# Rulers made ahead of the gathers, borders of edges in eight pieces, and another order of the last steps

## The chip, the core and the metric

The kernel runs on one core of a Trainium2 chip. The metric is the device time of one execution in microseconds (us). The engines of the core are PE (TensorE, matrix products; PEld is its weight load), DVE (VectorE), ACT (ScalarE), POOL (GpSimd) and SP (SyncE); each has a queue of its own and works through it in order. Transfers (DMAs) are issued by SP, ACT and POOL.

## The reference

A layer of a graph network over N = 12500 nodes of F = 128 features, with E = 212500 edges sorted by their target `dst`, and 8 heads of 16:

```python
h = maximum(layernorm(x), 0)
q = h @ Wq.T + bq;  k = edge_attr @ Wk.T + bk;  v = h @ Wv.T + bv
qs, qd = q[src], q[dst]
in_m, out_m, diag_m = sum(qs * k), sum(qd * k), sum(qs * qd)     # of each head
att = distance ** lam
score = (softmax over the edges of a node of in_m, out_m, diag_m, summed) * att
h = segment_sum(score[..., None] * v[dst], dst)
out = x + leaky_relu(h @ Wo.T + bo, 0.1)
```

So each edge needs the row of `q` of its source, which can be any of the 12500, and the row of `q` of its target, which lies near those of its neighbours in the list.

## The kernel before, in words

The edges lie in 416 blocks of 512. The list is cut into S = 5 stretches of G = 83 blocks (one block is left for the end); step g of the main loop does block t = g // 5 of stretch s = g % 5, so there are 415 steps (`end`). Three stages follow one another.

**First stage (lines 734 to 1014).** It makes `q` of all nodes, 98 tiles of 128 nodes in 25 groups of four. A loop over g from -2 to 34 does, for each group: `rectify` (ACT, line 921, four operations), `turn_h` (PE transposes, ACT copy, line 931), `nodes_q` (PE products, DVE sum, line 940, and SP's store of the group to `q_table`, line 942), then `ready` (mean and deviation to scale and shift) and `count_upto` (DVE statistics, line 886, eight groups ahead). Groups 25 to 34 are ten blocks of edges whose rows of `x` were gathered before `q` existed (`RAW`; 40 gathers on POOL, each behind a DVE instruction of its group). `side[g]` and the conditions on `r = g - GN` hang other work on the loop: the turning of sources and weights of edges, `edges_3` (the distance of each edge's target from the first of its block, line 832, and where each block begins), `edges_4` (borders between targets, lines 841 to 846), and `terms_of` (each `q` as a sum of three bfloat16 terms, nine units, lines 953 to 958; `put_terms` stores them, line 662). `show` makes rulers (constant patterns) from two POOL `iota`s (lines 752 and 755) and two DVE operations (757, 758). At g = 24 the gathers from `q_table` begin.

**Main loop (lines 1493 to 1552).** POOL gathers four times 128 rows of `q` for each step (`gather`, line 691), 20 steps ahead (`LOOK`) and behind the products of an earlier step. PE turns and projects the block's features (1154, 1163), spreads the targets' `q` from a window of 38 nodes (`win`, 645, and a one-hot matrix, 1171); DVE multiplies (1184, 1185) and adds up the heads (1190). One and two blocks later the softmax follows: `scan_on` (1244), `scan_back` (1262), `turn_max` (1332), `powers` (1340, 1341), `weigh_powers` (1352), `show_ends` (1366 to 1370), `to_rows` (PE, 1380) and `put_rows` (1396), which writes a stretch's 38 rows of sums to DRAM. Where the rows go is read into SP's registers by `fetch` (626). Pairs of finished nodes are completed on the way (`Nodes`).

**Last steps (lines 1555 to 1609).** Blocks 81, 82 and the odd one, 83, go through the softmax one after the other; then the sums of the last nine units (`rest`, five pairs; `load_sums`, lines 1061 and 1063) are read back, turned into scores together (`scores_of`, 1030 to 1036), and each pair is weighted with its `v` (`weigh`, 1096), turned (1080, 1083), multiplied with `Wo` (1088, 1107), added to `x` (1112, 1113) and stored (1119). `hold` computes `v` of a pair into a bank of PSUM. `last_pair` is a pair of nodes that is finished between.

The order of each engine is written out by hand: `pin` chains an instruction behind the one pinned before on the same engine:

```python
if engine in pinned:
    tc.add_manual_dep(inst.ins, pinned[engine], ... reason="in order")
pinned[engine] = inst.ins.name
```

What isn't pinned (the rulers of `show`, the register loads of `fetch`) is placed by the framework.

Of the kernel before, what the change touches and what calls it, by code (L numbers as in the profile page):

```python
# [21 lines left out]
FAR = 1e30  # L22
# [450 lines left out]
def ordered_path(ctx: ExitStack, tc: tile.TileContext, flag, x, src, dst, edge_attr, edge_weight,  # L473
# [144 lines left out]
    def fetch(t):  # L618

        if t >= T:  # L620
# [5 lines left out]
        _, base_v[t] = nc.values_load_multi_w_load_instructions(  # L626
            bases[0:1, t:t + (S - 1) * G + 1:G], engines=[mybir.EngineType.SP], min_val=0, max_val=N - 1,
            skip_runtime_bounds_check_because="the indices of nodes are below N")
        st[t] = dict(far=far)
# [104 lines left out]
    with tc.tile_pool(name="prep", bufs=1) as prep, \  # L734
# [14 lines left out]

        def show():  # L750
            of = prep.tile([K4, JN, S, W], F32, name="of_f", tag="of", bufs=2)
            nc.gpsimd.iota(of, pattern=[[1, JN], [JN, S], [0, W]], base=1, channel_multiplier=-1,
                           allow_small_or_imprecise_dtypes=True)
            row = prep.tile([1, JN, S, W], F32, name="of_row", tag="of", bufs=2)
            nc.gpsimd.iota(row, pattern=[[0, JN], [0, S], [1, W]], base=1, channel_multiplier=0,
                           allow_small_or_imprecise_dtypes=True)
            nc.vector.tensor_scalar(shows, of, 0.0, -1.0, op0=ALU.is_equal, op1=ALU.mult)
            nc.vector.tensor_copy(shows[0:1], row)
# [63 lines left out]
        def edges_2():  # L822
            turn_edges(weight, att_t)

        def edges_3():
            for i, lo in enumerate((1, BE, HEAD, 0)):
                pin(nc.vector.tensor_copy(marks[:, i], dst_r[:, lo:lo + (RB - 1) * BE + 1:BE]))
            pin(nc.sync.dma_start(base_d.rearrange("(r a) -> r a", a=RB),
                                  dst_r[:, 1:RC + 1:BE]))
            rel_b = of_tile().rearrange("r (a e) -> r a e", a=RB)  # L830
            for a in range(RB):
                pin(nc.vector.tensor_scalar(
                    rel_b[:, a].rearrange("r (j p) -> r p j", j=JN),
                    dst_r[:, 1 + a * BE:1 + (a + 1) * BE].rearrange("r (p j) -> r p j", j=JN),
                    marks[:, 0, a:a + 1], 1.0, op0=ALU.subtract, op1=ALU.add))
# [144 lines left out]
        for g in range(-2, GN + max(RAW, len(new) + 1)):  # L980
# [12 lines left out]
            if g in side:  # L993
                side[g]()
# [13 lines left out]
            if r == 3:  # L1008
                fetch_places(0)
# [645 lines left out]
```

## Time and profile before

| | |
|---|---|
| three runs | 2204.27, 2207.11, 2220.55 us; median 2207.11 |
| profiled execution | 2203.87 us, of which the span is 2201.3 us |
| busy | PE 78%, DVE 89%, ACT 64%, POOL 72% |
| granted clock of TensorE | 0.796 of full speed |
| gathers from `q_table` on POOL | 1620, from 85.8 us to 2128.1 us |
| products with gathered rows on DVE | 415, from 120.9 us to 2132.2 us |

A row of the timeline reads: start in us, duration in us, engine, line, operation, output and inputs, shapes, count of merged instructions, and in brackets how long the engine sat idle before it and what ended that. A row of the groups reads: busy time, mean ns of one, idle time before. A row of the windows gives for each engine its busy time in that stretch.

### The profile page before, as it was taken

How to read it: one execution, taken by the hardware profiler on the slowest of the kernel's cores; microseconds unless marked ns; L12 is line 12 of the kernel's file. 1: busy time of each engine (PE TensorE's matmuls, PEld its weight loads, DVE VectorE, ACT ScalarE, POOL GpSimd, SP SyncE). 2: the span in 40 equal slices, each digit the busy share in tenths (PEclk: the TensorE clock that was granted, in tenths of full speed). 3: DMA queues.
4: the chain of work that ended last, by engine and by line, in shares of the span. 5: the costliest groups of instructions: out<-in, count | busy, mean ns of one | idle time of the engine just before them, and what ended most of it. 6: DMA issues, size and time to landing. Idle time of an engine off the chain costs nothing.

```text
span 2201.3 us, 34508 instructions
## 1 busy us (share of the span) xinstructions
PE 1708.5 (78%) x10337; PEld 1362.8 (62%) x10337; DVE 1958.7 (89%) x2140; ACT 1414.6 (64%) x2639; POOL 1595.4 (72%) x1676
## 2 busy tenths in 40 slices
PE   6767777777778786888788778877877888788875
PEld 4545656566566665666666666666665666666664
DVE  7858999999888999989999999999999998988893
ACT  6846666666666666666666766666666666666671
POOL 5677777777777777777777777777777777777750
PEclk9867888878877878777877887787788777877877
DMA  9585554555554555545555554555556545544531
GB/s 260 170 255 152 168 164 148 175 149 162 173 155 146 157 166 176 160 148 156 175 168 154 183 170 147 158 180 157 156 166 183 150 147 164 162 148 145 161 91 58
DMA packets 306062, 355.66 MB, mean 162 GB/s; under 512 B 118195, under 2 KB 225661, under 8 KB 305557
## 3 DMA queue, kind: packets, MB, share of 16 engines
q1 hardware_dynamic: 237258, 238.26, 35.1%
q0 software_dynamic: 53184, 108.92, 17.1%
q10 hardware_dynamic: 15424, 6.19, 1.1%
q8 instruction: 83, 1.36, 0.3%
q14 instruction: 113, 0.93, 0.1%
HBM read 321.34 MB, written 31.85 MB: 160 GB/s over the span
## 4 chain that ended last, share of the span: by engine, by line
PE 37%; DVE 31%; DMA 11%; issue 9%; ACT 4%; POOL 2%; SPq 1%; ACTq 0%; DVEq 0%; POOLq 0%
PE kq_ps L1163 13%; DMA qq<-q_table,src_i 10%; DVE lT L1190 10%; DVE prod L1185 10%; PE w_ps L1380 6%; DVE prod L1184 5%; PE eT_ps L1154 5%; PE kq_ps L1161 4%; DVE u L1244 3%; PE node_ps L1088 3%; PE kq_ps L1171 3%; POOL qq L691 2%; PE d_ps L1366 2%; PE l_ps L1211 1%; ACT relb L1148 1%
## 5 line engine op out<-in xcount | busy, mean ns | idle before, releaser
L691 POOL DMA_INDIRECT qq<-q_table,src_i x1620 | 1547.1, 955 | 494.1 <-issue 233.9
L1163 PEld LDWEIGHTS kq_ps<-wk,eT 128*128 128x128 f32 x3320 | 522.2, 240 | 377.1 <-issue 159.4
L1190 DVE TENSOR_REDUCE lT<-prod 128x192 f32<-128x3072 f32 (+1 forms) x249 | 702.1, 2819 | 8.6
L1163 PE MATMUL kq_ps<-wk,eT 128*128 128x128 f32 x3320 | 617.5, 343 | 7.5 <-ACT eT L1156 6.5
L1174 ACT COPY qd<-kq_ps 128x512 f32<-128x512 f32 x415 | 242.2, 584 | 417.0 <-PE kq_ps L1171 386.0
L1185 DVE TENSOR_TENSOR prod<-qq,kq_ps 128x1024 f32<-128x1024 f32 x415 | 503.2, 1213 | 5.9 <-issue 3.2
L1161 PE MATMUL kq_ps<-b,ones 3*128 3x512 bf16 x415 | 185.6, 447 | 223.0 <-DVE prod L1185 222.8
L1154 PE MATMUL eT_ps<-ident,ea 128*128 128x128 f32 x1660 | 323.5, 330 | 1.0 <-DVE qq L940 1.0
L1148 ACT ACTIVATE relb<-relb,before 114x512 bf16<-114x512 bf16 x415 | 302.6, 729 | 0.0
L1184 DVE TENSOR_TENSOR prod<-qd,kq_ps 128x512 f32<-128x512 f32 x415 | 279.5, 674 | 12.0 <-ACT qd L1174 6.8
L1149 ACT ACTIVATE oh<-relb 114x512 bf16<-114x512 bf16 x415 | 261.4, 630 | 13.6 <-ACT relb L1148 0.4
L1156 ACT COPY eT<-eT_ps 128x512 f32<-128x512 f32 x415 | 244.0, 588 | 37.7 <-PE eT_ps L1154 37.2
L1154 PEld LDWEIGHTS eT_ps<-ident,ea 128*128 128x128 f32 x1660 | 229.1, 175 | 1.1 <-DVE qq L940 1.1
L1380 PE MATMUL w_ps<-back,sel 128*114 128x144 f32 (+1 forms) x1344 | 213.7, 320 | 19.3 <-DVE back L1352 14.8
L1380 PEld LDWEIGHTS w_ps<-back,sel 128*114 128x114 f32 (+1 forms) x1344 | 205.6, 211 | 26.4 <-ACT h L1070 9.2
L1332 PE MATMUL m_ps<-ident,m 120*128 120x120 f32 x332 | 70.9, 347 | 170.3 <-DVE m L1262 167.8
L1171 PE MATMUL kq_ps<-win,oh 114*128 114x128 bf16 x1660 | 199.9, 255 | 2.6 <-DMA win<-q_table 2.6
L1341 ACT ACTIVATE back<-back 128x480 f32<-128x480 f32 x83 | 50.1, 604 | 201.9 <-DVE back L1340 201.9
L1244 DVE TENSOR_TENSOR_SCAN u<-far,u,l_ps 120x512 f32<-120x512 bf16 x82 | 104.7, 1276 | 78.2 <-PE l_ps L1211 77.0
L1171 PEld LDWEIGHTS <-oh 114*128 114x128 bf16 x1660 | 161.2, 118 | 15.5 <-issue 2.8
L1332 PEld LDWEIGHTS m_ps<-ident,m 120*128 120x128 f32 x332 | 50.7, 215 | 192.8 <-DVE m L1262 188.6
L1262 DVE TENSOR_TENSOR_SCAN m<-far_ps,head,u 120x512 f32<-120x512 f32 x81 | 103.1, 1273 | 0.0
(192 smaller groups left out, 1467.4 us busy)
## 6 DMA issues: line engine op xcount, KB each, us to landing
ea<-in_edge_attr_dram SPq DMA_DIRECT2D x83, 1280.0 KB
relb<-rel_d SPq DMA_DIRECT2D x83, 640.0 KB
qq<-q_table,src_i POOLq DMA_INDIRECT x1620
win<-q_table SPq DMA_DIRECT2D x415, 28.5 KB
far<-far_d SPq DMA_DIRECT2D x84, 120.2 KB
q_table<-more_q SPq DMA_DIRECT2D x40, 192.0 KB
sums<-rows SPq DMA_DIRECT2D x412, 7.1 KB
q_table<-xq SPq DMA_DIRECT2D x24, 256.0 KB
```

What stands on the lines that cost most here:

```text
L691: rows = pin(nc.gpsimd.indirect_dma_start(out=qq[:, j, :], out_offset=None, in_=x if g < RAW else q_table, in_offset=bass.IndirectOffsetOn ...
L1148: pin(nc.scalar.activation(d, d, AF.Abs, bias=before[:K3]))
L1149: pin(nc.scalar.activation(oh, d, AF.Relu, bias=1.0, scale=-1.0))
L1154: pin(nc.tensor.transpose(eT_ps[:, j, :], eas[g // S][:, g % S, j * F:(j + 1) * F], ident))
L1156: pin(nc.scalar.copy(eT, eT_ps))
L1161: pin(nc.tensor.matmul(k_ps, ones3, bk3, start=True, stop=False))
L1163: pin(nc.tensor.matmul(k_ps[:, j, :], eTs[g][:, j, :], wk, start=False, stop=(j == JN - 1)))
L1171: pin(nc.tensor.matmul(qd_ps[:, j, :], ohs[g][:, j * P:(j + 1) * P], d["win"][:, s, :], start=(j == 0), stop=(j == JN - 1)))
L1184: pin(nc.vector.tensor_mul(prod[:, :, 2, :], qds[g], kqs[g][:, 0]))
L1185: pin(nc.vector.tensor_mul(prod[:, :, 0:2, :], qqs[g][:, :, None, :].to_broadcast([P, JN, 2, F]), kqs[g].rearrange("p i j f -> p j i f")))
L1190: pin(nc.vector.tensor_reduce(lTs[t][:, :, lo:s + 1, :].rearrange("p j s c -> p j (s c)"), prods[0][:, :, :s + 1 - lo].rearrange("p j s i ...
L1380: pin(nc.tensor.matmul(w_ps[:, i].rearrange("p s c -> p (s c)"), d["sel"][:n, j, lo:lo + 3, :].rearrange("p s w -> p (s w)"), d["back"][:n ...
```

## The change

First stage: both `iota`s of the rulers are issued before the first gather, and the two DVE operations that use them are pinned. `edges_3` and `edges_4` are cut into four pieces each, one for each quarter of a row of blocks; one piece is issued at each g from 11 that has no other side work (11, 12, 14, 15, 18, 20, 21, 22). What ACT does for the borders (`edges_5`) comes at g = 24, the check of order (`edges_6`) at the end of the stage. The turning of weights (`edges_2`) is spread over four g. `fetch_places(0)` and `fetch(0)` come at r = 0. The tile `q3` gets five buffers for three, and its second cast moves from ACT to DVE.

Main loop: the window of the first block is fetched before the borders of the second. In the last five steps `select` and `show_ends` of the last three blocks are issued one a step; `v` of the first pair of `rest` and the turning of `last_pair` are issued in the last two steps. The register loads are pinned, and for the last three blocks ACT loads them too.

Last steps: `hold`, `powers`, `weigh_powers` and `to_rows` stand in another order; every second `put_rows` of the last three blocks is issued by ACT; `last_pair` gets its scores before the sums are loaded, and its end (`add_x`, with the sum on POOL) follows later; the scores of `rest` are made in two parts, of two pairs and of three.

```diff
@@ fetch
-        _, base_v[t] = nc.values_load_multi_w_load_instructions(
-            bases[0:1, t:t + (S - 1) * G + 1:G], engines=[mybir.EngineType.SP], ...
+        at = [mybir.EngineType.SP] + [mybir.EngineType.Activation] * (t >= G - 2)
+        loads, base_v[t] = nc.values_load_multi_w_load_instructions(
+            bases[0:1, t:t + (S - 1) * G + 1:G], engines=at, ...
+        for load_of in loads:
+            pin(load_of)
@@ first stage
+        of_f = prep.tile([K4, JN, S, W], F32, name="of_f", tag="of", bufs=2)
+        nc.gpsimd.iota(of_f, ...)
+        of_row = prep.tile([1, JN, S, W], F32, name="of_row", tag="of", bufs=2)
+        pin(nc.gpsimd.iota(of_row, ...))
+
         def show():
-            of = prep.tile([K4, JN, S, W], F32, name="of_f", tag="of", bufs=2)
-            nc.gpsimd.iota(of, ...)
-            row = prep.tile([1, JN, S, W], F32, name="of_row", tag="of", bufs=2)
-            nc.gpsimd.iota(row, ...)
-            nc.vector.tensor_scalar(shows, of, 0.0, -1.0, op0=ALU.is_equal, op1=ALU.mult)
-            nc.vector.tensor_copy(shows[0:1], row)
+            pin(nc.vector.tensor_scalar(shows, of_f, 0.0, -1.0, op0=ALU.is_equal, op1=ALU.mult))
+            pin(nc.vector.tensor_copy(shows[0:1], of_row))
...
-        def edges_2():
-            turn_edges(weight, att_t)
-        def edges_3():
...
-        def edges_4():
...
+        def edges_2(which):
+            turn_edges(weight, att_t, which)
+        def edges_3(a):
+            if a == 0:
+                for i, lo in enumerate((1, BE, HEAD, 0)):
+                    pin(nc.vector.tensor_copy(marks[:, i], dst_r[:, lo:lo + (RB - 1) * BE + 1:BE]))
+                pin(nc.sync.dma_start(base_d.rearrange("(r a) -> r a", a=RB),
+                                      dst_r[:, 1:RC + 1:BE]))
+                made["rel"] = of_tile().rearrange("r (a e) -> r a e", a=RB)
+            pin(nc.vector.tensor_scalar(made["rel"][:, a]..., dst_r[:, 1 + a * BE:1 + (a + 1) * BE]...,
+                marks[:, 0, a:a + 1], 1.0, op0=ALU.subtract, op1=ALU.add))
+            if a == RB - 1:
+                pin(nc.sync.dma_start(rel_d.rearrange("(r a) e -> r a e", a=RB), made["rel"]))
+                pin(nc.sync.dma_start(bases, base_d[None, :]))
+        def edges_4(a):
+            if a == 0:
+                made["cuts"] = of_tile()
+            part = slice(a * BE, (a + 1) * BE)
+            pin(nc.vector.tensor_tensor(made["cuts"][:, part], dst_r[:, 1:][:, part], dst_r[:, part],
+                                        op=ALU.is_gt))
+        def edges_5():
             far_b = of_tile()
-            pin(nc.scalar.mul(far_b, cuts, -FAR))
+            pin(nc.scalar.mul(far_b, made["cuts"], -FAR))
...
+        def edges_6():
+            pin(nc.vector.scalar_tensor_tensor(of_tile(), dst_r[:, 1:], 0.0, dst_r[:, :RC], op0=ALU.add,
                                                op1=ALU.is_lt, accum_out=worst))
...
-                q3 = q3s[u] = node.tile([P, 2, 3, F], BF, name="q3", bufs=3)
+                q3 = q3s[u] = node.tile([P, 2, 3, F], BF, name="q3", bufs=5)
...
-                pin(nc.scalar.copy(q3[:, :, 1, :], q))
+                pin(nc.vector.tensor_copy(q3[:, :, 1, :], q))
...
+        pieces = [(edges_3, a) for a in range(RB)] + [(edges_4, a) for a in range(RB)]
...
             if g in side:
                 side[g]()
+            elif g >= 11 and pieces:
+                f, a = pieces.pop(0)
+                f(a)
...
                 gather_few()
-                edges_3()
+                edges_5()
...
-            if r == 3:
+            if r == 0:
                 fetch_places(0)
-            if r == 4:
-                edges_4()
                 fetch(0)
-            if r == 6:
-                edges_2()
+            if 2 <= r < 2 + RB:
+                edges_2([r - 2])
+            if r == len(new):
+                edges_6()
@@ main loop
-            sel = st[t]["sel"] = work.tile([P, JN, S, W], F32, name="sel", bufs=3)
+            sel = st[t]["sel"] = work.tile([P, JN, S, W], F32, name="sel", bufs=4)
...
-                    pin(nc.sync.dma_start(
+                    pin((nc.scalar if t >= G - 2 and s % 2 else nc.sync).dma_start(
...
+        fetch_rows(0)
         fetch(1)
-        fetch_rows(0)
...
+            if t == G - 2 and 0 < s < 3:
+                select(G - 2 + s)
             if t == G - 1:
-                if 0 < s < 4:
-                    select(G - 3 + s)
-                elif s == 4:
-                    for i in (G - 2, G - 1, G):
-                        show_ends(i)
+                if s == 0:
+                    select(G - 2)
+                    show_ends(G - 1)
+                elif s == 1:
+                    show_ends(G)
+                elif s == 2:
+                    show_ends(G - 2)
...
+            if g == end - 2:
+                hold(rest[0], True)
+            if g == end - 1:
+                last_pair.turn(small([P, JN, P], "node_ps"))
+                more_banks()
@@ last steps
         turn_logits(G - 1)
-        last_pair.scores()
-        last_pair.turn(small([P, JN, P], "node_ps"))
+        last_pair.project_v(banks.pop(0))
         scan_on(G - 1)
-        hold(rest[0], True)
-        more_banks()
-        last_pair.project_v(banks.pop(0))
         scan_back(G - 2)
+        hold(rest[1])
         turn_max(G - 2)
         scan_on(G)
+        powers(G - 2)
         scan_back(G - 1)
         turn_max(G - 1)
+        weigh_powers(G - 2)
         scan_back(G)
         turn_max(G)
-        for t in (G - 2, G - 1, G):
-            powers(t)
-        for t in (G - 2, G - 1, G):
-            weigh_powers(t)
-        last_pair.weigh(last_pair.held)
-        for t in (G - 2, G - 1, G):
+        to_rows(G - 2)
+        powers(G - 1)
+        powers(G)
+        weigh_powers(G - 1)
+        weigh_powers(G)
+        put_rows(G - 2)
+        for t in (G - 1, G):
             to_rows(t)
             put_rows(t)
+        last_pair.scores()
+        last_pair.weigh(last_pair.held)
         for r, of in enumerate(rest):
             of.load_sums(ends_ab[:, r * JN:r * JN + of.n], of.more)
-        hold(rest[1])
...
-        last_pair.add_x(nc.vector)
-        last_pair.store()
...
+        end_scores(0, 2)
         for r in range(len(rest) + 2):
             if r < len(rest):
                 rest[r].weigh(rest[r].held)
+            if r == 1:
+                last_pair.add_x(nc.gpsimd)
+                last_pair.store()
+                end_scores(2, len(rest))
...
-                rest[r - 2].add_x(nc.vector)
+                rest[r - 2].add_x(nc.gpsimd if r == 2 else nc.vector)
```

`end_scores(lo, hi)` adds the second part of the sums of pairs lo to hi - 1 (DVE, the operation of line 1596) and calls `scores_of` for their tiles alone.

53 lines of the change are left out of this document (21 added, 32 removed).

## The prediction

> **What bounds the kernel now.** I read the page's totals first, then the tile view of `qq`, then what DVE waits for late in the main loop, then the timelines of the first 120 us and the last 75 us.
>
> ```profile
> PE 1708.5 (78%) x10337; PEld 1362.8 (62%) x10337; DVE 1958.7 (89%) x2140; ACT 1414.6 (64%) x2639; POOL 1595.4 (72%) x1676
> L691 POOL DMA_INDIRECT qq<-q_table,src_i x1620 | 1547.1, 955 | 494.1 <-issue 233.9
> ...
> L691 POOL DMA_INDIRECT qq<-q_table,src_i x1620: 940/947/2766, 85.8 to 2128.1; - x180
> L1185 DVE TENSOR_TENSOR prod<-qq,kq_ps x415: 1201/1212/1222, 120.9 to 2132.2; 128x1024 f32<-128x1024 f32 x139
> ...
> DVE prod L1185 <- DMA qq<-q_table,src_i: 2.5, 1, 2.5
> DVE prod L1185 <- issue: 1.5, 1, 1.5
> ```
>
> DVE looks like the bound at 89%, and POOL, at 72%, does not. But POOL's idle time is 494.1 / 1620 = 0.305 us ahead of each gather, so a gather costs 0.955 + 0.305 = 1.26 us, and 1620 of them take 2041 us: they run from 85.8 to 2128.1 us without a break. The last product starts 4.1 us behind the last gather, the first one 35 us behind the first. So DVE, a little quicker than four gathers a step (5.04 us), catches up during the loop and late in it waits for rows (the last two lines, from 1800 to 2100 us). It waits little, 4 us: there the two have the same pace, and an earlier stream is worth its full gain only if DVE starts earlier too. The loop's end is **the start of the gather stream plus 2041 us**. What the change does in the middle is hidden; two places count: what sets the start at 85.8 us, and the 73 us after 2128.1 us.
>
> ```profile
> 18.11 1.13 POOL L755 IOTA of_row<- 1x760 f32 x1
> 19.28 0.55 DVE L758 CAST shows<-of_row 1x760 bf16<-1x760 f32 x1 [6.66 <-POOL of_row L755]
> 19.75 2.20 DVE L886 BATCH_NORM_STATS2 stats<-xq 128x6 f32<-128x128 f32 x11
> ...
> 23.82 1.65 ACT L921 ACTIVATE xq<-xq,shift,inv 128x128 f32<-128x128 f32 x4 [0.82 <-DVE shift L909]
> ...
> 68.35 11.28 SPq L942 DMA_DIRECT2D q_table<-xq  x7
> ...
> 80.53 4.80 DVE L832 TENSOR_SCALAR of<-dst_r,marks 104x512 bf16<-104x512 int32 x4
> 80.76 4.69 POOL L691 DMA_INDIRECT qq<-in_x_dram,raw_i  x1 [0.30 <-issue]
> 85.76 0.95 POOL L691 DMA_INDIRECT qq<-q_table,src_i  x1 [0.31 <-DMA base_d<-dst_r]
> ...
> 96.57 2.28 DVE L841 TENSOR_TENSOR of<-dst_r 104x2048 bf16<-104x2048 int32 x1
> 97.78 1.89 POOL L691 DMA_INDIRECT qq<-q_table,src_i  x1 [0.30 <-issue]
> 100.88 2.29 DVE L846 SCALAR_TENSOR_TENSOR of<-dst_r 104x2048 bf16<-104x2048 int32 x1 [2.03 <-ACT of L843]
> 101.23 2.77 POOL L691 DMA_INDIRECT qq<-q_table,src_i  x1 [0.30 <-issue]
> ...
> 24.00:48.00 24.00, 22.20 (x133) 17.96 (x134) 19.75 (x85) 23.91 (x62) 11.24 (x12) 1.00 0.85 213
> 48.00:80.26 32.26, 28.50 (x185) 21.43 (x182) 27.98 (x120) 31.26 (x83) 15.02 (x17) 1.00 0.71 235
> 80.26:114.00 33.74, 22.89 (x123) 18.33 (x122) 25.99 (x64) 25.99 (x65) 27.34 (x22) 0.80 0.53 136
> ...
> GB/s 260 170 255 152 168 164 148 175 149 162 173 155 146 157 166 176 160 148 156 175 168 154 183 170 147 158 180 157 156 166 183 150 147 164 162 148 145 161 91 58
> ...
> xq<-in_x_dram SPq DMA_DIRECT2D x5, 896.0 KB
> L957 ACT CAST q<-xq 128x256 bf16<-128x256 f32 x9 | 3.7, 407 | 0.7 <-DVE xq L954 0.6
> ```
>
> Two things hold the start. DVE stands still for 6.66 us because the second ruler is queued on POOL behind eleven gathers; statistics, and ACT with them, wait. And the last gather from `x` takes 4.69 us for 0.95, and ends at 85.45 us just as DVE's four operations of line 832 do (80.53 + 4.80): while these run POOL does not get on. The gathers beside lines 841 and 846 are stretched in the same way.
>
> **The change part by part: the start.** *Rulers ahead.* POOL is free before its first gather, whose indices come from DVE, so the 1.13 us cost nothing there. The wait of 6.66 us goes. Line 757, until now done early, joins 758, so I take 5.9 us. Whether the features are there 6 us sooner the trace doesn't show; bounds 0 and 6.7. Ahead of the tiles that DVE takes next lie 1.8 MB of pieces of `x` (0.9 MB the last) and 0.6 MB of gathers, 9 us at the 260 GB/s of the page's first slice, so they should be. ACT is then the limit to 48 us (23.91 of 24), and keeps the 5.9 us.
>
> *Eight pieces.* They add to DVE, from g = 11 on (about 48 us now), 4.80 for line 832, 2.28 and four small overheads for 841 and 0.4 for the marks: 7.7 us. The window from 48 to 80.26 us has 32.26 - 27.98 = 4.3 us of idle DVE. So DVE becomes the limit of that stretch and ends it 3.4 us later; bounds 0 (other pauses are used) and 7.7 (none is). Net, `q` is complete 5.9 - 3.4 = 2.5 us sooner. The lock of 3.7 us falls among gathers from `x`, which are paced by DVE and have room (15.02 of 32.26 us). The last of the seven stores to `q_table` is issued near 79.3 us now (they end at 68.35 + 11.28) and would be at 77; the stream starts about 80.5 instead of 85.76: **5 us sooner** (3 to 9).
>
> *Within the stream.* Line 841's stretch (1.89 - 0.95) goes, line 846 stays (at the end of the stage) with its 1.8. The nine second casts, 0.41 us each on ACT, become casts on DVE among gathers; the trace has none there. Bounds: 0, and for each the 1.8 us that line 846 cost; I take 0.1 each, since the gathers beside short DVE operations keep 0.95 us. Sum: 0. I leave **0.5 us** as gain.
>
> *The later part of the first stage.* ACT loses 3.7 us of casts and its waits behind lines 832 and 841, and the first window no longer waits for a transfer and five registers:
>
> ```profile
> 114.61 0.76 SPq L625
> ...
> 115.41 1.57 SPq L626
> ...
> 117.21 1.85 DMA win<-q_table
> ```
>
> ACT's 25.99 us without 3.7 are 22.3, plus pauses: the stage ends near 104 us instead of 114, and with 2.4 us from SP's order the first product starts some 12 us sooner. This is more than the stream gains, so the loop stays bound by gathers and only the 5.5 us count. Five buffers, spread turning and `fetch` at r = 0 (SP waits there for the borders to land) lie within it: nothing. In the loop, 15 register loads on ACT cost three times 1.57 us, as on SP, in steps where DVE waits for rows: nothing; uncovered 4.7.
>
> **The last steps.**
>
> ```profile
> 2135.89 1.39 PE L1366 MATMUL d_ps<-shows,ends_t 21*128 21x380 bf16 x3
> ...
> 2139.06 0.65 PE L1211 MATMUL l_ps<-ident,lT 128*120 128x128 f32 x4
> ...
> 2149.51 8.36 PE L1380 MATMUL w_ps<-back,sel 128*114 128x144 f32 x48 [0.60 <-DVE back L1352]
> ...
> 2154.56 7.87 SPq L1396 DMA_DIRECT2D sums<-rows  x15
> ...
> 2162.08 4.80 ACTq L1063 DMA_DIRECT2D qq<-sums  x7
> 2162.48 5.60 SPq L1061 DMA_DIRECT2D ends_ab<-sums  x9
> ...
> 2170.31 0.69 DVE L1112 TENSOR_TENSOR h<-h,node_ps 128x512 f32<-128x512 f32 x1 [14.77 <-ACT h L1107]
> ...
> 2171.64 1.96 DVE L1596 TENSOR_TENSOR ends_ab<-ends_ab,qq 128x384 f32<-128x384 f32 x4
> ...
> 2179.36 0.69 DVE L1096 TENSOR_TENSOR qq<-eT_ps,end_score 128x512 f32<-128x512 f32 x1
> ...
> 2185.30 0.69 DVE L1112 TENSOR_TENSOR qq<-qq,node_ps 128x512 f32<-128x512 f32 x1 [4.06 <-ACT qq L1107]
> ...
> 2193.56 0.43 DVE L1113 TENSOR_TENSOR qq<-qq 128x256 f32<-128x256 f32 x1
> ...
> 2158.88 1.32 SPq L626
> 2163.79 3.15 DMA qq<-sums
> ```
>
> *Softmax.* Between 2135.89 and 2139.06 us PE steps through three `show_ends` in turn with ACT; that goes into steps bound by gathers. But PE then has `hold` of two pairs and the turning of `last_pair` ahead of what DVE waits for, and it runs now fast, now at half speed. Laid out by these rows, `to_rows` ends 6 us sooner with PE fast all along and 2 us later with PE slow: I take 1.5 sooner.
>
> *Rows out and in.* SP's 15 stores take 7.87 us, 1.32 of it a register load that moves back to its `fetch`. With two of five on ACT and block 81 well ahead, what follows the last block's rows shrinks by 2 us (0 to 3).
>
> *Scores.* The sums of the first two pairs, the first four on SP, are there at about 2162.48 + 3 x 0.62 + 3.15 = 2167.5 us; DVE begins at 2171.64, since the end of `last_pair` is ahead of it in its queue (14.77 us idle) and waits for ACT's seven issues. Four sums and the scores of 18 tiles take until 2179.36 us, 1.96 + 5.76; two sums and 8/18 of the scores come to 1.0 + 2.6 = 3.6 us. So DVE weighs the first pair at 2171.1, 8 us sooner, and does the other scores in the pause of 4.06 us in which it now waits for PE. Its work from 2171.64 to 2193.99 is then 22.35 - 4.06 = 18.3 us; POOL takes one sum, the maximum of `last_pair` comes in, and a second set of short operations adds 0.4: 18.7. From 2167.5 that ends at 2186.2, with 0.8 us of waits for PE at 2187. **7 us** (5 to 9). The two sums on POOL are waited for by stores alone.
>
> Together 1.5 + 2 + 7 = 10.5 us, and with 5.5 of the start **16 us**: the profiled execution, 2203.87 us (the span and 2.6 us around it), would take 2187.9 us. It lies 3.2 us below the median of the runs, so the median would be 2207.1 - 16 = 2191 us.
>
> **A rule against it.** The gathers that ended with line 832 and were stretched by 841 and 846 show that DVE's work can hold up POOL's. The Trainium skill, SBUF — State Buffer, section Who interferes with whom, says that casts and `tensor_scalar` may take a port pair that DVE shares with GpSimd, exclusively for the whole instruction, and starve descriptors of gathers, while `tensor_tensor` does not. By that rule the moved casts lock the stream and the pieces of 841 never did; this trace agrees on line 832 (4.69 us) and differs on 841 (1.89 us).
>
> **The rivals.** *Casts stall the stream.* Nine casts on DVE, in the gather stream, each holding POOL as lines 832 and 846 did: 9 x 1.8 = 16 us at most, 5 as likely when a cast is a quarter as long as 846. For it: three such rows. Against: the casts are short. Price 4 to 16 us: 2195 to 2207.
>
> *The pieces cost what they save* (ends on the other side). From g = 11 on DVE and ACT are both nearly full (27.98 and 31.26 of 32.26 us), and a late DVE makes ACT late, which then makes PE and DVE wait. If the pieces delay `q` by twice their length, 15.4 us for 3.4, the stream starts at 80.5 + 12 = 92.5, 6.7 us later than now; with PE slow at the end (10.5 - 6.5 = 4 us gained) and 5 us of stalls by casts that gives 2207 + 6.7 + 5 - 4 = 2215. It decides from 13 us of delay on, where the start loses 4. Against: the statistics run eight groups ahead.
>
> *The end doesn't shrink.* The three `show_ends` ask for six more of the three small PSUM buffers in steps 410 to 412, whose holders wait for DVE's scans; PE, in order, stands still and the products come late. Two steps of 4 us would leave 16 - 8: 2199.
>
> *More than said.* DVE's pieces all fit (3.4 us more), PE fast at the end (4.5 more): 24 us, 2183.
>
> **How the numbers follow.** The forecast with its terms' bounds, 2186 to 2197, gets 0.52; casts 0.13; the short end 0.12; more than said 0.17; the pieces 0.06. The range that leaves out less than 0.2 is 2181 to 2203. One per cent, 22 us, is about what a measurement of this kernel can tell from no change; faster by more needs under 2185, which is the fourth rival and a corner of the forecast: 0.22. Slower by more, over 2229, is a corner of the pieces: 0.04. Within: 0.74.
>
> **What would show it.** No POOL wait of line 758; first gather from `q_table` near 80.5 us and none longer than 2 us but beside line 846; DVE full from 43 to 78 us; first product near 109 us; last gather 5 us sooner, last product right behind it; first weighing of a pair some 20 us before the end. The prediction is wrong if the stream starts after 84 us or before 77, if the gathers at lines 953 to 958 are stretched, or if the last `to_rows` ends more than 30 us behind the last gather.

## The result, and the profile after

The changed kernel takes **2194.16 us** (median of seven runs, 2190.63 to 2200.47) and the kernel before, measured beside it, 2207.11 (seven runs, 2201.46 to 2222.61). The medians differ by 13.0 us. The ratio is 0.9934, 95% interval 0.9914 to 0.9954, which is 14.6 us less, 10 to 19. The forecast was 2191 and 16 us less. The sum holds; its two parts don't, as the experiments show.

The profiled execution is the slowest of the seven, 2200.47 us with a span of 2198.7. First its page, totals and groups:

```profile
PE 1711.7 (78%) x10337; PEld 1367.5 (62%) x10337; DVE 1964.1 (89%) x2156; ACT 1411.1 (64%) x2630; POOL 1591.9 (72%) x1678
...
L694 POOL DMA_INDIRECT qq<-q_table,src_i x1620 | 1542.7, 952 | 496.7 <-issue 245.3
...
L1260 DVE TENSOR_TENSOR_SCAN u<-far,u,l_ps 120x512 f32<-120x512 bf16 x82 | 104.7, 1277 | 95.9 <-PE l_ps L1227 89.8
```

and the view of the tile `qq` (first and last start behind the three durations):

```profile
L694 POOL DMA_INDIRECT qq<-q_table,src_i x1620: 940/945/2572, 84.7 to 2122.1; - x180
L1201 DVE TENSOR_TENSOR prod<-qq,kq_ps x415: 1200/1214/1217, 112.2 to 2139.4; 128x1024 f32<-128x1024 f32 x139
```

The busy shares say nothing of the change. The tile's rows do. The stream starts 1.1 us sooner (85.8) and not 5, and ends 6.0 us sooner (2128.1). The first product comes 8.7 us sooner (120.9), but **the last one 7.2 us later** (2132.2), 16 us behind the last gather, where the prediction had it right behind. So in this execution DVE was the late one, and the last row of the page's groups above shows where it waited most: 95.9 us ahead of the scan, 89.8 of them for PE's turned logits. The same row of the kernel before, which the prediction left out, had 78.2:

```profile
L1244 DVE TENSOR_TENSOR_SCAN u<-far,u,l_ps 120x512 f32<-120x512 bf16 x82 | 104.7, 1276 | 78.2 <-PE l_ps L1211 77.0
```

The first 110 us as a timeline, and its windows (busy time of PE, PEld, DVE, ACT, POOL, then PE's granted clock, DMA share, GB/s):

```profile
2.84 1.48 POOL L757 IOTA of_row<- 1x760 f32 x1
...
11.15 0.54 DVE L762 CAST shows<-of_row 1x760 bf16<-1x760 f32 x1
...
13.59 2.21 DVE L898 BATCH_NORM_STATS2 stats<-xq 128x6 f32<-128x128 f32 x11
...
43.67 0.68 DVE L952 TENSOR_TENSOR xq<-q_ps,bq_all 128x512 f32<-128x512 f32 x1
...
48.61 1.37 DVE L836 TENSOR_SCALAR of<-dst_r,marks 104x512 bf16<-104x512 int32 x1
48.72 1.55 POOL L694 DMA_INDIRECT qq<-in_x_dram,raw_i  x1 [0.30 <-issue]
...
54.58 1.01 SPq L833 DMA_DIRECT2D base_d<-dst_r  x1
55.70 3.11 SPq L954 DMA_DIRECT2D q_table<-xq  x4
59.38 0.34 SPq L841 DMA_DIRECT2D rel_d<-of  x1
66.16 0.23 SPq L842 DMA_DIRECT2D bases<-base_d  x1
...
72.66 7.38 SPq L954 DMA_DIRECT2D q_table<-xq  x7
...
78.46 0.41 DVE L952 TENSOR_TENSOR xq<-q_ps,bq_all 128x256 f32<-128x256 f32 x1
...
80.38 0.95 POOL L694 DMA_INDIRECT qq<-in_x_dram,raw_i  x1 [0.30 <-POOLq L803]
84.65 0.94 POOL L694 DMA_INDIRECT qq<-q_table,src_i  x1 [3.32 <-ACT hT L943]
...
98.77 1.14 POOL L694 DMA_INDIRECT qq<-q_table,src_i  x1 [0.30 <-issue]
...
105.39 2.57 POOL L694 DMA_INDIRECT qq<-q_table,src_i  x1 [0.30 <-issue]
```
```profile
42.00:78.00 36.00, 29.26 (x182) 22.49 (x181) 33.59 (x124) 30.43 (x79) 15.86 (x16) 0.95 0.90 231
78.00:110.00 32.00, 23.90 (x137) 18.89 (x137) 23.36 (x73) 25.30 (x61) 22.03 (x22) 0.85 0.60 184
```

The same two sums of `q` before (the twelfth of 25 and the last):

```profile
49.40 0.68 DVE L940 TENSOR_TENSOR xq<-q_ps,bq_all 128x512 f32<-128x512 f32 x1
...
78.83 0.41 DVE L940 TENSOR_TENSOR xq<-q_ps,bq_all 128x256 f32<-128x256 f32 x1
```

The wait of DVE for the second ruler is gone and the statistics stand 6.2 us earlier (13.59 for 19.75). At the twelfth sum of `q` the stage is still 5.7 us ahead (43.67 for 49.40); then come the pieces, and at the last sum 0.4 us is left (78.46 for 78.83). The gather that took 4.69 us takes 0.95. Yet POOL then stands still for 3.32 us. The releaser that this row names had ended before; what came last by the semaphores of the trace were the last stores of `q`. The last three, issued at 78.3, 78.8 and 79.4 us, took 4.5 to 4.7 us each to land, the last until 83.9 us. In the kernel before the last one was issued at 79.3 us too and landed at 81.0, 1.7 us later.

The last steps:

```profile
2112.78 1.21 DVE L1201 TENSOR_TENSOR prod<-qq,kq_ps 128x1024 f32<-128x1024 f32 x1
...
2123.60 0.66 PE L1096 MATMUL node_ps<-ident,qq 128*128 128x128 f32 x4 [2.63 <-ACT sel L1385]
...
2139.36 1.21 DVE L1201 TENSOR_TENSOR prod<-qq,kq_ps 128x1024 f32<-128x1024 f32 x1
...
2161.18 0.40 ACT L1401 COPY rows<-w_ps 114x288 f32<-114x288 f32 x1 [1.74 <-PE w_ps L1396]
...
2165.79 0.56 DVE L1623 TENSOR_TENSOR ends_ab<-ends_ab,qq 128x384 f32<-128x384 f32 x1 [5.80 <-DMA ends_ab<-sums]
2167.86 0.56 DVE L1623 TENSOR_TENSOR ends_ab<-ends_ab,qq 128x384 f32<-128x384 f32 x1 [1.51 <-DMA ends_ab<-sums]
...
2171.64 0.69 DVE L1112 TENSOR_TENSOR qq<-eT_ps,end_score 128x512 f32<-128x512 f32 x1
...
2184.32 0.69 DVE L1128 TENSOR_TENSOR qq<-qq,node_ps 128x512 f32<-128x512 f32 x1 [3.18 <-ACT qq L1123]
...
2190.69 0.43 DVE L1129 TENSOR_TENSOR qq<-qq 128x256 f32<-128x256 f32 x1
```

The first and the third row are the products of steps 409 and 414. From the last rows copied to DVE's last operation it is 2191.1 - 2161.6 = 29.5 us, and was 2194.0 - 2158.3 = 35.7 (2157.95 us and 0.40 for that copy before).

### The profile page after: what moved, and what is told of

Read it like the earlier page. It is cut to its first block, busy times and chain, and to the rows that moved or that the text cites. A ratio compares the mean times of both kernels' runs of the same rounds, so it can differ in the third digit from the quotient of the medians.

```text
span 2198.7 us, 34525 instructions
## 1 busy us (share of the span) xinstructions
PE 1711.7 (78%) x10337; PEld 1367.5 (62%) x10337; DVE 1964.1 (89%) x2156; ACT 1411.1 (64%) x2630; POOL 1591.9 (72%) x1678
## 4 chain that ended last, share of the span: by engine, by line
PE 38%; DVE 29%; DMA 12%; issue 10%; ACT 6%; POOL 3%; SPq 1%; DVEq 0%; ACTq 0%; POOLq 0%
PE kq_ps L1179 14%; DMA qq<-q_table,src_i 11%; DVE prod L1201 9%; DVE lT L1206 8%; PE w_ps L1396 6%; PE eT_ps L1170 5%; DVE prod L1200 5%; PE kq_ps L1177 4%; POOL qq L694 3%; PE kq_ps L1187 3%; DVE u L1260 3%; PE node_ps L1104 3%; PE d_ps L1382 1%; ACT eT L1172 1%; PE l_ps L1227 1%
## 5 line engine op out<-in xcount | busy, mean ns | idle before, releaser
L1396 PEld LDWEIGHTS w_ps<-back,sel 128*114 128x114 f32 (+1 forms) x1344 | 208.9, 214 | 29.5 <-ACT h L1086 11.9
L1260 DVE TENSOR_TENSOR_SCAN u<-far,u,l_ps 120x512 f32<-120x512 bf16 x82 | 104.7, 1277 | 95.9 <-PE l_ps L1227 89.8
```

The costliest lines, as they stand in the source:

```text
L1396: pin(nc.tensor.matmul(w_ps[:, i].rearrange("p s c -> p (s c)"), d["sel"][:n, j, lo:lo + 3, :].rearrange("p s w -> p (s w)"), d["back"][:n ...
```

## The experiments

The first four runs were made on a chip where the kernel before takes 2206.85 us. The other eight were made on a second one, where PE's granted clock is 0.74 to 0.75 and **the kernel before takes 2695 us**; their times are compared there only. The kernel before has no profile on that chip.

**Each half alone.** The first stage of the changed kernel with the last steps of the old, and the reverse.

> First stage of the changed kernel (rulers, pieces, casts, first rows), last steps of the kernel before. Two theories of the loop. Gathers: it ends with the last gather from q_table plus 3 us. Products: it ends 2011 to 2027 us behind the first product (the lengths in the two profiles), whatever the gathers do, since DVE waits for PE on the way. Both see the stream start near 84.7 us and the first product near 112 us, as in the changed kernel's profile, and 69 us from the last product to the end, as before. Gathers: last product near 2126 us, 2197 us in all. Products: last product between 2123 and 2139 us, 2194 to 2210 us, the middle 2202, with the last product 5 us or more behind the last gather.

> First stage of the kernel before, last steps of the changed one. Both theories see the stream start at 85.8 us, the first product at 121 us and 59 to 62 us from the last product to the end (59.3 in the changed kernel's profile, 69.1 in that of before). Gathers: last product near 2132 us, 2193 to 2196 us in all. Products: last product between 2132 and 2148 us, 2193 to 2210 us, the middle 2202. If the first stage is worth nothing this takes what the changed kernel takes, 2194 us.

First stage alone: 2196.36 us, ratio 0.9965 (0.9948 to 0.9981). Last steps alone: 2202.37 us, 0.9976 (0.9959 to 0.9994). By the ratio and by the medians that is 8 to 11 us for the first stage and 4 to 5 for the last steps; I had said 5.5 and 10.5. The two tile views, first stage alone and then last steps alone, and with the first the products of steps 409 and 414 from its timeline:

```profile
L691 POOL DMA_INDIRECT qq<-q_table,src_i x1620: 940/944/1899, 83.3 to 2121.4; - x180
L1198 DVE TENSOR_TENSOR prod<-qq,kq_ps x415: 1201/1212/1217, 111.3 to 2130.0; 128x1024 f32<-128x1024 f32 x139
```
```profile
2107.05 1.22 DVE L1198 TENSOR_TENSOR prod<-qq,kq_ps 128x1024 f32<-128x1024 f32 x1
...
2129.96 1.21 DVE L1198 TENSOR_TENSOR prod<-qq,kq_ps 128x1024 f32<-128x1024 f32 x1
```
```profile
L694 POOL DMA_INDIRECT qq<-q_table,src_i x1620: 940/944/3061, 86.2 to 2126.5; - x180
L1188 DVE TENSOR_TENSOR prod<-qq,kq_ps x415: 1200/1212/1217, 121.8 to 2148.7; 128x1024 f32<-128x1024 f32 x139
```

Both have products late at the end, by 8 and 21 us, which "gathers" excludes. The profiled time minus the start of the last product is 2197.4 - 2130.0 = 67.4 us with the old last steps (71.7 before) and 61.4 with the new (61.1 in the changed kernel). What differs between these profiles besides is how long the products take from the first to the last. The last five steps take 22.9 us with the old last steps (2129.96 - 2107.05) and 26.6 both in the changed kernel (2139.36 - 2112.78) and with the last steps alone.

**Which chain sets the loop's end.** The gathers from `q_table` held back, and the products held back:

```diff
@@ gather_late
             if r == -1:
-                for b in range(RAW, LOOK):
-                    gather(b)
-                gather_few()
                 edges_5()
...
+            if r == 3:
+                for b in range(RAW, LOOK):
+                    gather(b)       # the first one also waits for DVE's work of that group
+                gather_few()
@@ products_late
                 edges_6()
+                for _ in range(8):
+                    pin(nc.vector.tensor_add(xq[:, 0:8, :], xq[:, 0:8, :], xq[:, 8:16, :]))
```

> The changed kernel with its stream of gathers from q_table held back by four groups of the first stage, about 10 us, and DVE, ACT and PE as they were. Gathers: 2194 + 10 = 2204 us, last product 3 us behind the last gather. Products: the lag of 16 us between last gather and last product shrinks to 6, the time stays within 0 to 4 us of the changed kernel's, 2194 to 2198.

> The changed kernel with eight more sums of 128x1024 on DVE between the first stage and the first product, 8 x 1.21 = 9.7 us, whose results nobody uses; the stream of gathers starts as it did. Gathers: DVE catches up, 2194 to 2197 us. Products: the whole delay is kept, 2204 us, and the last product lies 10 to 26 us behind the last gather.

Gathers late: 2200.02 us (2196.95 to 2203.01); products late: 2203.98 us (2189.31 to 2215.06).

```profile
L694 POOL DMA_INDIRECT qq<-q_table,src_i x1620: 940/944/2567, 92.0 to 2130.3; - x180
L1210 DVE TENSOR_TENSOR prod<-qq,kq_ps x415: 1200/1212/1222, 111.8 to 2136.2; 128x1024 f32<-128x1024 f32 x139
```
```profile
L694 POOL DMA_INDIRECT qq<-q_table,src_i x1620: 940/944/2572, 82.6 to 2122.3; - x180
L1203 DVE TENSOR_TENSOR prod<-qq,kq_ps x415: 1200/1212/1222, 120.5 to 2128.3; 128x1024 f32<-128x1024 f32 x139
```
```profile
L1262 DVE TENSOR_TENSOR_SCAN u<-far,u,l_ps 120x512 f32<-120x512 bf16 x82 | 104.7, 1277 | 67.6 <-PE l_ps L1229 60.7
```

(The last row is from the groups on the page of the kernel with late products.) The stream came 7.3 us later (10 were intended) and the time rose by 5.9; the first product came 8.3 us later and the time rose by 9.8. Each theory alone expected one of the two to be nearly free, and **neither was**. The lengths say why. On this chip the gathers took 2038 to 2043 us in all six profiles. From first to last product it took 2011.2 (before), 2027.2 (changed kernel), 2018.7 (first stage alone), 2026.9 (last steps alone), 2024.4 (gathers late) and 2007.8 us (products late); the last of these, with the scan waiting 67.6 us, is also the fastest run of its kernel (2189.31 us), and the 2026.9 the slowest of its (2210.10).

Which chain is late can be seen inside each profile. This is the time from the end of a step's fourth gather to the start of its product, in us:

| profile | step 40 | step 200 | step 320 | step 400 | step 414 |
|---|---|---|---|---|---|
| before | 67.0 | 40.5 | 12.1 | 4.8 | 3.1 |
| changed kernel | 59.1 | 32.5 | 20.1 | 16.2 | 16.3 |
| first stage alone | 62.2 | 25.2 | 17.8 | 11.2 | 7.6 |
| last steps alone | 68.4 | 36.0 | 26.3 | 21.2 | 21.3 |
| gathers late | 55.3 | 17.7 | 3.4 | 4.0 | 5.0 |
| products late | 67.0 | 34.8 | 10.9 | 3.4 | 5.1 |

DVE catches up in every profile, and no gather of the stream (with the odd block's two) starts more than 0.42 us behind the end of the one before, so the stream never waits for DVE. Where the lag has come down to 3 to 5 us it stays there: from about step 320 on with late gathers, from about 360 on in the kernel before and with late products. There the rows hold the products. In the other three the lag never gets that small, and the products hold the end. So the loop ends with the later of two chains of almost equal length, and the length of one of them differs by 20 us between the profiles. It goes with DVE's wait ahead of the scan: 67.6 and 78.2 us in the two shortest, 93.7 to 95.9 where the products hold the end.

Taken as a bare maximum, with the median run of the changed kernel ending its products at 2194.2 - 61.1 = 2133 us, the late gathers should cost 3 us (they end at 2131.2, and the last product lies 5 us behind in that profile) and the late products 8. The measured 5.9 and 9.8 us (8 and 12 by the ratios) are higher, and their intervals (3 us for the one, 4 for the other, 4 for the changed kernel) only just allow the 3 us. The maximum explains that both delays come through; how much of each comes through, these runs don't settle.

**Moving the waits of DVE.** The scan one step behind its transposes, and the cast of a later unit one step ahead; and the same with the borders' transfers behind the last store of `q`.

```diff
@@ scan_later
                 if t > 0:
                     turn_logits(t - 1)
-                    scan_on(t - 1)
...
             elif s == 1:
+                later(scan_on, t - 1)
                 later(scan_back, t - 2)
@@ other_terms
-            elif s == 2:
-                q3 = held["q3"] = work.tile(...)
-                pin(nc.scalar.copy(q3[:, :, 0, :], held["q"]))
+            elif s == 1:
+                held["q3"] = work.tile(...)
+                pin(nc.scalar.copy(held["q3"][:, :, 0, :], held["q"]))
+            elif s == 2:
                 pin(nc.vector.tensor_sub(...))
@@ scan_borders, besides: edges_3 only computes, edges_5 begins with its three transfers
+            pin(nc.sync.dma_start(base_d..., dst_r[:, 1:RC + 1:BE]))
+            pin(nc.sync.dma_start(rel_d..., made["rel"]))
+            pin(nc.sync.dma_start(bases, base_d[None, :]))
```

> The changed kernel with two waits of DVE for others moved out of its way: the scan of a block is issued one step later than the transposes that feed it (DVE waited there 73 to 101 us in the profiles so far), and the cast of a later unit one step ahead of the subtraction that needs it (49 to 53 us). If the loop ends with the later of two chains, the gathers (stream start + 2038 to 2043 us, last product 3 us behind) and the products (first product + 2008 to 2027 us), the second falls below the first: last product 3 to 5 us behind the last gather in this profile, every run within 4 us of each other, 2188 to 2192 us. If the products lag for another reason (ACT, PSUM), nothing changes: 2194 us, runs 10 us apart. Gathers alone: 2194 us as well, with the lag at 3 us.

> As the run with the scan a step later, and the three transfers of the borders (start of each block, distances, and the load of the starts, which waits 6.3 us on SP for the first of them to land) moved behind the last store of q, where the kernel before had them. Expected: the last seven stores of q take 1.7 us each again instead of 4.5, the stream starts 2 to 3 us sooner (81.5 to 82.5 us for 83 to 84.7), and since the loop is bound by gathers now, the time falls by as much, 2186 to 2189 us. If the products still bind, or the first product comes later by what the borders are late (2 to 8 us), it stays at or above the other run's time.

> The run with the scan a step later once more, beside the changed kernel. Near a clock of 0.80: if waits of DVE for PE in the scan are what lets the products fall behind the gathers, last product 3 to 6 us behind the last gather, 2188 to 2192 us with little spread; if PE itself is what is late, the waits move to other operations of DVE as they did at 0.746 (from the scan to the subtraction of the maximum) and the time stays at the changed kernel's, 2194 us. Near 0.745: the changed kernel's time within 3 us.

> The changed kernel itself beside the others of this call. On a chip with a granted clock near 0.80: stream start 82.5 to 85 us, first product 111 to 112.5 us, last product at the later of stream start + 2038 to 2043 us (+3) and first product + 2008 to 2027 us, 59 us from there to the end, 2190 to 2200 us, 0.993 of the kernel before. On one near 0.745, where the kernel before took 2696 us: last product 95 us behind the last gather, 50 to 52 us from the last product to the last operation of DVE, and, if the gain of the last steps is all that is left there, 0.996 to 0.998 of the kernel before.

The second chip: the changed kernel 2697.83 us, 1.0007 (0.9988 to 1.0026) of the kernel before, so **there the change is worth nothing** (0.996 to 0.998 was expected). The scan a step later: 2689.64 us, 0.9979 (0.9957 to 1.0001), and measured again, beside the changed kernel, 2689.62 us, 0.9973 (0.9958 to 0.9988). With the borders' transfers moved as well: 2689.49 us, 0.9979 (0.9962 to 0.9996). The groups of DVE, changed kernel first, then the scan a step later (the second measurement):

```profile
L1200 DVE TENSOR_TENSOR prod<-qd,kq_ps 128x512 f32<-128x512 f32 x415 | 279.8, 674 | 36.7 <-ACT qd L1190 23.9 <-ACT sel L1386 4.2 <-issue 3.8
L1260 DVE TENSOR_TENSOR_SCAN u<-far,u,l_ps 120x512 f32<-120x512 bf16 x82 | 104.9, 1280 | 244.8 <-remote 104.1 <-PE l_ps L1227 58.5 <-PE kq_ps L1179 47.6
...
L1356 DVE TENSOR_TENSOR back<-lT,m_ps 128x480 f32<-128x480 f32 x83 | 54.2, 653 | 214.2 <-PE m_ps L1348 95.9 <-remote 61.4 <-PE kq_ps L1179 24.6
```
```profile
L1200 DVE TENSOR_TENSOR prod<-qd,kq_ps 128x512 f32<-128x512 f32 x415 | 281.6, 679 | 251.7 <-ACT qd L1190 195.4 <-issue 48.6 <-ACT rows L1402 3.0
L1260 DVE TENSOR_TENSOR_SCAN u<-far,u,l_ps 120x512 f32<-120x512 bf16 x82 | 104.3, 1271 | 0.4 <-remote 0.2
```

244.8 us of waiting at the scan become 0.4, and the product's wait grows from 36.7 to 251.7: the wait moves. The product now waits for ACT's copy `qd`, and that copy itself stood idle for 758.2 us, 398.5 of them until a releaser that the profile can't place ("remote"). Where the two chips differ most is PE's group of line 1179, here of the changed kernel on the first chip and on the second:

```profile
L1179 PE MATMUL kq_ps<-wk,eT 128*128 128x128 f32 x3320 | 617.3, 343 | 9.1 <-ACT eT L1172 8.0
```
```profile
L1179 PE MATMUL kq_ps<-wk,eT 128*128 128x128 f32 x3320 | 678.6, 368 | 476.4 <-ACT eT L1172 240.1
```

PE stood idle ahead of these products for 9.1 us there and for 476.4 here, about as much as the kernel is slower. That PE is what is late on this chip fits these rows; what makes it stand still is not shown. The gathers follow: the lag of the table above is 113 to 125 us in all eight profiles of this chip at every step from 40 to 380, and 20 steps take 120 there. That is as far ahead as `LOOK` lets them go, so here POOL waits for the products, and by this reading an earlier stream gains nothing.

8 us are left as gain of the later scan over the changed kernel (the two intervals touch at 0.9988). Against the kernel before, one of its two measurements is clear of no change and the other just isn't. It wasn't run near a clock of 0.80; whether it brings the loop down to the gathers there stays open.

With the borders' transfers behind it, the last store of `q` is issued at 80.97 us, lands 2.5 us later, and the stream starts at 84.5, 3.5 us behind the issue. The six profiles of this chip with the same first stage and the transfers early have 2.7 to 5.5 us there, landings of 1.6 to 4.7 us, and starts from 82.5 to 86.8. So it isn't shown that the transfers cost the stream anything; the start I expected, 81.5 to 82.5 us, did not come. The time is the same as without that edit, as must be where the products end 96 us behind the gathers.

**Single terms.** Only the rulers ahead; the matrices of the last blocks back in the loop's last step, or earlier; one set of scores.

```diff
@@ rulers_only: the kernel before with both iotas ahead of the gathers, their two users pinned
@@ shows_last                          @@ shows_early (sel has five buffers)
-  s == 0: show_ends(G - 1)            -  t == G - 1, s == 0: show_ends(G - 1)
-  s == 1: show_ends(G)                -  t == G - 1, s == 1: show_ends(G)
-  s == 2: show_ends(G - 2)            +  t == G - 3, s == 4: show_ends(G - 1)
+  s == 4: all three                   +  t == G - 2, s == 4: show_ends(G)
                                       (select of both blocks also goes from t == G - 2 to G - 3)
@@ scores_once
-        end_scores(0, 2)
+        end_scores(0, len(rest))
...
-                end_scores(2, len(rest))
```

> The kernel before with the two rulers ahead of the gathers and nothing else. My prediction put 5.9 us on it. The statistics of the third group of tiles start near 13.6 us for 19.75, and q is complete and the stream starts 4 to 6 us sooner only if the lock of the last gather from x beside the four operations on the borders (4.69 us) moves with it: stream start 80 to 82 us, first product 115 to 117 us, 2201 to 2203 us. If transfers or ACT take the gain back: stream start 84 to 86 us, 2205 to 2208 us.

> The changed kernel with the matrices of the last three blocks (three times two products on PE and three operations on ACT) made in the loop's last step, as before, and no longer one block a step in steps 410 to 412. If these make the last steps late, the last five take 23 us as in the run with only the first stage changed, and not 26.6; behind the loop PE and ACT then need 2 to 3 us more ahead of the softmax. Expected: the same time within 2 us, 2192 to 2196 us: what the loop's end gains, the last steps lose. If the place in the loop is free, this run is 2 to 3 us slower than the changed kernel.

> The changed kernel with two of the three extra blocks of matrices taken out of the last five steps: those of block 82 in step 404, of block 83 in step 409, of block 81 in step 412 as before (a fifth buffer for them). If four such blocks in four successive steps (410 to 413) are what made the last five steps 26.6 us instead of 22.9, they take 23 to 24 us where the products bind, and the time from the last product to the end stays: 2 to 3 us less than the changed kernel. If the pace of the last steps is PE's clock alone, no difference.

> The changed kernel with the scores of all five pairs made at once again, nothing else. In the changed kernel the first weighing comes 10.1 us behind the last rows copied and the last operation of DVE 19.3 to 19.5 us behind that. Expected: the first weighing 5 to 7 us later (five sums and five pairs of scores instead of two), the last operation of DVE 2 to 4 us later than in the changed kernel, counted from the last rows. If the split is worth my 7 us in whole: 6 to 7 us later. If the second set of scores only moves the wait: the same.

Rulers alone: 2688.91 us, 0.9979 (0.9957 to 1.0002). The last store of `q` is issued at 78.5 us, the gather beside line 832 takes 4.72 us and the stream starts at 85.0, so the lock decides still: my 80 to 82 is refuted, and 84 to 86 holds, though not for the reason given with it (transfers or ACT). Its median is 9 us below the changed kernel's, but the intervals overlap.

Shows last: 2699.09 us, 1.0012 (0.9995 to 1.0028). Shows early: 2695.04 us, 0.9989 (0.9973 to 1.0006). Both intervals overlap the changed kernel's. The last five steps take 26 to 28 us in these and in the changed kernel on this chip (23 and 23 to 24 expected), and 26.2 with the old last steps (rulers alone). So whether the place of the matrices explains the 3.7 us of the first chip stays open. Made last, they cost behind the loop: the last rows come 30.5 us behind the last product, for 22.2.

One set of scores: 2698.41 us, 1.0010 (0.9991 to 1.0028), no difference in time either, but its trace sizes the split: the first weighing at 2670.10 us, 15.5 behind the last rows, and the end of DVE's last operation at 2685.4, 30.8 behind them, against 10.2 and 29.5 in the changed kernel on that chip. So the first weighing comes 5.3 us sooner by the split (5 to 7 expected), and the end 1.3 (2 to 4 expected).

```profile
2654.22 0.40 ACT L1401 COPY rows<-w_ps 114x288 f32<-114x288 f32 x1 [1.74 <-PE w_ps L1396]
...
2670.10 0.69 DVE L1112 TENSOR_TENSOR qq<-eT_ps,end_score 128x512 f32<-128x512 f32 x1
...
2684.99 0.42 DVE L1129 TENSOR_TENSOR qq<-qq 128x256 f32<-128x256 f32 x1
```

## Why the prediction was right, and where it was not

The time is right because two errors cancelled, which is luck: the start of the products gained more than I counted, the stream's start and the last steps less. Two of the three signs that I had named for being wrong are there in the profile: the stream starts after 84 us (84.65), and the last `to_rows` ends more than 30 us behind the last gather (2161.1 for 2123.1 us).

*"The loop's end is the start of the gather stream plus 2041 us."* This step failed. The length is right (2038.4 us), but the end is that of the later of two chains. In three of the six profiles near a clock of 0.80 the last product lies 8 to 21 us behind the last gather, in the other three 3 to 5. I read DVE's short waits for rows late in the profile of before as a bound; it was one execution in which the two chains met, at about step 360 of 415. The products' chain holds waits for PE (78.2 us ahead of the scan in that profile), and the sum had no term for how they vary.

*Rulers, 5.9 us.* Right: 6.2 us at the statistics, and 5.7 still at the twelfth sum of `q`.

*Eight pieces, 3.4 us of loss.* Mis-sized: 5.7 us ahead become 0.4, so they cost 5.3 us here, and 4.1 to 5.6 in the four profiles of this first stage near a clock of 0.80. DVE was nearly full, as forecast (33.59 of 36 us). The bounds, 0 to 7.7, hold. No run on that chip has the rulers without the pieces. On the second chip it takes 32.5 us from the twelfth sum to the last with the rulers alone and 34.2 to 36.1 in the seven profiles with the whole first stage, so there the pieces, and what else the stage changed, cost 1.7 to 3.5.

*"The stream starts about 80.5."* Failed: 84.7, 83.3 and 82.6 us in three profiles. The lock went as forecast: the last gather from `x` ends at 81.33 us and not at 85.45. But besides the pieces, the step left out SP's queue and the transfers: the load of the starts (66.16 us) waits on SP, from 59.7 us on, until their store (54.58 us) has landed, the stores of `q` behind it pile up, at the issue of the last one five are under way, and the last three take 4.5 to 4.7 us where the last one took 1.7. What the lock's going gave, their landing took. That the borders' transfers are what made the landing long was not shown: the run that moved them has a stream start amid those without.

*First product 12 us sooner.* 8.7 to 9.6 us, and this was worth more than "hidden": the first stage alone gave 8 to 11 us, where the 5.5 of the stream were counted.

*Casts, 0.1 us each.* Right. Among the gathers between 85 and 105 us four are longer than 0.97 us (1.09, 1.18, 1.14, 1.09): 0.7 us in all in the stretch of the nine casts, and the first two of the four have no cast beside them but a `tensor_tensor` of line 970. Line 846's operation kept its stretch (2.57 us for 0.95), as forecast. The rule that I weighed against the change, from the Trainium skill, SBUF — State Buffer, section Who interferes with whom, that one of the two engines blocks the other for a whole instruction, agrees with a quarter of line 832 (a `tensor_scalar` of 1.37 us, the gather beside it 1.55 us for 0.94). For the casts the trace doesn't show it: the nine take 2.8 us together, and the gather at 91.27 us took 0.95 us with a whole cast of 0.28 us inside it.

*Last steps, 10.5 us.* Too much: 4 to 5. From the last rows on, 6.2 us instead of 9 were gained: the first weighing came 11 us sooner, as far behind the rows as forecast, but DVE waits 3.18 and 1.22 us for the later pairs. "In the pause of 4.06 us in which it now waits for PE" is the phrase that failed: the pause moved behind the second set of scores. Splitting them is worth 1.3 us on the second chip (30.8 less 29.5); what gave the rest, the end of `last_pair`, ACT's stores or something else, no run separates. And the rival *the end doesn't shrink* happened in part: the last five steps take 26.6 us with the new last steps and 22.9 with the old, 3.7 us of the 8 that I priced. PE waits for ACT's `sel` in between (2123.60 us), but that the three `show_ends` cost the 3.7 us is not shown: with them out of these steps, on the second chip, the steps still take 27.1.

*The pieces cost what they save* and *casts stall the stream* did not happen on the first chip. On the second, where the gain is gone, the forecast has no term for what holds the kernel.

## What to carry to other kernels

When a profile shows two engines at nearly the same pace, hold back each by a known amount: if both delays come through, neither is the bound alone, and an edit has to move both starts. A lag between them that is read along the whole loop shows in one profile which of the two is late, and since when. When a stall goes, ask when the next input lands: work that is moved takes its transfers along, into the queue of those that matter. A tail gains only what its last chain loses; filling a pause with work of the same engine moves the pause.

## What the runs showed of the hardware

The same program took 2207 us on one chip and 2695 on another, with PE's granted clock at 0.80 and 0.74 to 0.75, and DVE's busy time nearly the same (1964.1 and 1972.7 us in the changed kernel). On the second chip PE stood still for long stretches: in the window from 110 to 170 us of the changed kernel it was busy for 16.8 of 60 us at a granted clock of 0.56. Around that window DVE stands still for 55.2 us in two waits ahead of sums of `q`, which read PE's products; the releaser is one that the profile can't place. The first product came there at 166 to 171 us in the seven profiles with the new first stage and at 155 in the one with the rulers alone. Why it comes 11 to 16 us later there with the new first stage, and 9 us sooner near a clock of 0.80, was not settled.

```profile
110.00:170.00 60.00, 16.81 (x80) 13.25 (x81) 14.16 (x34) 13.71 (x33) 25.70 (x28) 0.56 0.22 64
```
